# Queries and keys of an attention stage formed by seven half-block products instead of eight full ones, with the work around them reordered

## The chip, the core and the metric

The kernel runs as one program on one core of a Trainium2 chip. The metric is the device time in microseconds; three runs of the kernel before gave 2507.08, 2508.03 and 2508.86 us, median 2508.03. All data is float32. The engines are called as the profile calls them: PE (TensorE: the matrix products, with PEld for its weight loads), DVE (VectorE), ACT (ScalarE), POOL (GpSimd) and SP (the engine that issues most transfers).

## The reference

Four layers act on `x` of 128 x 64 x 256 (batch, node, feature) with one adjacency matrix of 64 x 64. Each adds its result to `x`; each starts with a layer norm and a relu. The first is a graph convolution followed by small LSTMs, the second is attention, the third a graph layer with two batch norms, the fourth three graph convolutions. Only the attention matters here:

```python
qkv = h @ W                                   # h: relu(layernorm(x)), W: 256 x 768
q, k, v = ...                                 # four heads of 64
mask = jnp.where(adj == 0, -jnp.inf, 0.0)
scores = einsum('bhid,bhjd->bhij', q, k) / np.sqrt(64) + mask
attn = jax.nn.softmax(scores, axis=-1)
x = x + einsum('bhij,bhjd->bhid', attn, v)
```

## The kernel before, in words

The 8192 tokens (128 batches of 64 nodes) are cut into 16 groups (`NG`) of 512 tokens (`GN`). The program is written engine by engine through a tile layer: within an engine the instructions run in the order in which the layer issues them, engines wait for each other by semaphores, and `tc.issue_after(...)` says that what follows may not be issued ahead of a named instruction. All products go through eight PSUM banks from one pool (`psp`, `bank()`).

**The attention loop** (L843 to L892) takes one group for each turn `g`, with pieces of neighbouring groups between:

- `to_residual(g + 3)` (L236, transposes at L246, additions at L250) brings the first layer's result of a later group into `xs`, by way of a copy `hc` made half by ACT and half by POOL (L239).
- `queries_keys(hT)` (L735) multiplies the transposed features `hT` (256 features on 2 x 128 partitions, 512 tokens) by the 256 x 512 weights `wqk`: four output tiles of 128 x 512, two products each, eight products 512 columns wide (L744), and ACT copies each result into `q` or `k` (L748).
- `values(hT, v, (0,))` and later `(1,)` (L760, copy L766) make the values, 16 narrow products for each half.
- `turn(e)` (L808, copies L811) transposes the exponentials of the group before.
- `features(transposed(h))` (transposes L124, copies by DVE at L258) makes the `hT` of the next group.
- `attend` (L821) makes the outputs of the group before, and `softmax` (L768) the scores of this group (L779), mask and scale (L786), maximum (L793), subtraction (L794), the exponential on ACT (L795), and their sums and reciprocals on DVE (L798, L799).
- `add_output(g - 1)` (L833 on DVE, L836 on POOL) divides by the sums and adds to `xs`; `normalized(g + 2)` (bn_stats L90, L92, L93, the power on POOL at L94, L96, the four activations L109 on ACT) prepares a later group's `h`.

After group 15 the loop's last turn runs into the third layer: `mixed` (L141) and `hidden` (L716), whose weights `w1` come by a transfer (L863) into the place of `wqk`.

**The seven-product form** exists already in the kernel: the LSTM gates and the fourth layer use it. A product of two matrices, each cut into 2 x 2 blocks, is formed from seven block products instead of eight; `sums` and `differences` form the combined blocks, four tensor operations each, and `seven` (L159) issues the products in the order 1, 5, 6, 7 into four banks. ACT copies products 1 and 5 to `p1`, `p5` (L169, L170), DVE adds products 6 and 7 to these (L172, L173), and then `finish` adds p1 and p5 on POOL for one output block (L176) and issues products 2, 3 and 4 on top of banks whose first contents have been read. One block is then read out by ACT (L210), two by DVE (L181, L185).

**Before the attention** come the LSTM steps. In the last of them `w_att` is loaded with the attention's weights (L668), and group 0's `hT` is made between LSTM products (L683). The last LSTM output `h` is written at L538, after a tanh at L530.

Of the kernel before, what the change touches and what calls it, by code (L numbers as in the profile page):

```python
# [14 lines left out]
P = 128  # L15
D = 256
# [22 lines left out]
def adj_preln_kernel(ctx: ExitStack, tc: tile.TileContext, x_in, adj, vec, bg0, bg1,  # L39
# [9 lines left out]
    def bank(shape=(P, 512)):  # L49
        return psp.tile(list(shape), F32, tag="ps", name="ps")  # L50
# [68 lines left out]
    def transposed(src):  # L119

        pss = [bank() for _ in range(2)]
        for c in range(2):
            for t in range(GT):
                nc.tensor.transpose(  # L124
                    pss[c][:, t * P : (t + 1) * P], src[:, t, c * P : (c + 1) * P], ident
                )
        return pss
# [32 lines left out]
    def seven(products, banks, p1, p5, out, end, parts=lambda b: [b]):  # L160

        ps = banks
        for i, p in zip((1, 5, 6, 7), ps):
            products[i](p, True)
        nc.scalar.copy(p1, ps[0])  # L169
        nc.scalar.copy(p5, ps[1])  # L170

        nc.vector.tensor_tensor(p1, p1, ps[2], ALU.add)  # L172
        nc.vector.tensor_tensor(p5, p5, ps[3], ALU.add)  # L173

        def finish():
            nc.gpsimd.tensor_tensor(out=out[1][1], in0=p1, in1=p5, op=ALU.add)  # L176
            end(1, 1, None)
            products[2](ps[0], False)
            end(0, 0, ps[0])
            products[3](ps[1], False)  # L180
            nc.vector.tensor_tensor(out[0][1], p1, ps[1], ALU.add)  # L181
            end(0, 1, None)
            products[4](ps[3], False)
            for to, p, q in zip(*(parts(b) for b in (out[1][0], p1, ps[3]))):
                nc.vector.tensor_tensor(to, p, q, ALU.add)  # L185
                end(1, 0, None, to)

        return finish

    def differences(eng, b11, b12, b21, b22, t1, t2, t3, t4, negate=False):  # L190
# [61 lines left out]

    keep = ctx.enter_context(tc.tile_pool(name="keep", bufs=1))

    def features(pss, k):

        for c in range(2):
            nc.vector.tensor_copy(hTs[:, k, c, :], pss[c])  # L258
        return hTs[:, k]

    with tc.tile_pool(name="lw", bufs=5) as lw:

# [201 lines left out]
        with tc.tile_pool(name="back", bufs=1, reuse_waits="tile") as back_pool, \  # L464
# [183 lines left out]
            for p, nk in ((1, 8), (2, 8), (3, 7), (4, 8)):  # L648
                n = nk * HB
                wi, wh = w_next  # L650
                if p < 4:
                    w_next = (load_w(wih, p), load_w(whh, p))
                starts = range(0, NODES // p // nk * nk, nk)
                units = [(tiles, k0) for tiles in ((0, 1), (2, 3)) for k0 in starts]

                for j in range(0, len(units), 2):
                    two = [unit(p, *u, nk) for u in units[j : j + 2]]
                    first_steps(p, n, two, units[j : j + 2], w0)
                    if p > 1:
                        flush()  # L660
                        if j == 0:
                            ws = blocks_of(p, wi, wh)
                    if j + 2 == len(units):
                        if p < 4:
                            w0 = first_blocks(w_next[0], weight_tile())
                        else:
                            w_att = weight_tile()
                            nc.sync.dma_start(  # L668
                                out=w_att[:, :, 0:768], in_=wqkv.rearrange("(c p) f -> p c f", p=P)
                            )  # L670
                            wqk, wv = w_att[:, :, 0:512], w_att[:, :, 512:768]
                    for t in range(1, p):
                        for i, u in enumerate(two):
                            next_step(t, p, n, u, ws)

                            if p == 4 and j == 2 and 2 * t + i - 2 < NK:
                                to_residual(2 * t + i - 2, xs[2 * t + i - 2], back_pool, 1)
                            if p == 4 and j == 2 and t == p - 1 and i == 0:

                                h = back_pool.tile([P, GT, D], F32, tag="hc", name="h")  # L680
                                ln_relu(xs[0], h)
                                hTs = keep.tile([P, 2, 2, GN], F32, tag="arena", name="hT")
                                hT = features(transposed(h), 0)  # L683

    xpool_b = ctx.enter_context(tc.tile_pool(name="xres_b", bufs=1, reuse_waits="tile"))
    for g in range(NK, NG):
# [42 lines left out]
    with tc.tile_pool(name="att", bufs=2, reuse_waits="tile") as ap_:  # L729
# [2 lines left out]
            ln_relu(xs[g], h)  # L732
            return h

        def queries_keys(hT):  # L735

            qk = []
            for s, tag in enumerate(("q", "k")):
                dst = ap_.tile([P, 2, GN], F32, tag=tag, name=tag)
                for m in range(2):  # L740
                    ps = bank()
                    col = s * D + m * P
                    for c in range(2):
                        nc.tensor.matmul(  # L744
                            ps, lhsT=wqk[:, c, col : col + P], rhs=hT[:, c, :],
                            start=(c == 0), stop=(c == 1),
                        )
                    nc.scalar.copy(dst[:, m, :], ps)  # L748
                qk.append(dst)
            return qk  # L750

        def values(hT, v, ks):

# [14 lines left out]
        def softmax(qT, kT):  # L768


            e = ap_.tile([P, 2 * GT, 2, NODES], F32, tag="e", name="e")
            pss = [bank((P, 2 * GT, NODES)) for _ in range(2)]
            for t in range(GT):
                for m in range(2):
                    for b in range(2):
                        tok = t * P + b * NODES
                        for par in range(2):
                            rows = slice(par * 64, par * 64 + 64)
                            nc.tensor.matmul(  # L779
                                pss[par][b * 64 : b * 64 + 64, 2 * t + m, :],  # L780
                                lhsT=qT[rows, m, tok : tok + NODES],
                                rhs=kT[rows, m, tok : tok + NODES],
                                start=True, stop=True,
                            )
            for par in range(2):
                nc.vector.scalar_tensor_tensor(  # L786
                    e[:, :, par, :], pss[par], 0.125,
                    mask.unsqueeze(1).to_broadcast([P, 2 * GT, NODES]), ALU.mult, ALU.add,
                )
            ef = e.rearrange("p a q j -> p (a q) j")  # L790
            NH = 4 * GT
            mx = ap_.tile([P, NH, 1], F32, tag="mx", name="mx")
            nc.vector.tensor_reduce(mx[:, :, 0], ef, AX.X, ALU.max)  # L793
            sub = nc.vector.tensor_tensor(ef, ef, mx.to_broadcast([P, NH, NODES]), ALU.subtract)  # L794
            nc.scalar.activation(ef, ef, AF.Exp)  # L795
            ri = ap_.tile([P, 2 * GT, 2, 1], F32, tag="ri", name="ri")
            rif = ri.rearrange("p a q o -> p (a q o)")
            nc.vector.tensor_reduce(rif, ef, AX.X, ALU.add)  # L798
            nc.vector.reciprocal(rif, rif)  # L799
            return e, ri, sub.ins  # L800

        def turn(e):

# [34 lines left out]

        h = normalized(1)
        last = None
        for g in range(NG + 1):  # L843
            if 0 < g <= NG - NK:
                to_residual(g + NK - 1, xs[g + NK - 1], ap_, 1)
            if g == NG - NK + 1:
                hres_pool.__exit__(None, None, None)
                with tc.using_default_side("right"):
# [6 lines left out]
                    mixed(i, (on_scalar, on_scalar))  # L855
                hidden(0, w1, range(2))
            if g < NG:
                q, k = queries_keys(hT)
                if g == NG - 1:

                    w1 = w_att[:, :, 0:512]
                    w2 = w_att[:, :, 512:1024].rearrange("p a (b f) -> a p b f", f=D)
                    nc.sync.dma_start(out=w1, in_=w1t.rearrange("(c p) f -> p c f", p=P))  # L863
                v = ap_.tile([P, 2 * GT, P], F32, tag="v", name="v")
                values(hT, v, (0,))
            if last is not None:
                e, ri, v_last = last
                eT, turned = turn(e)
# [1 line left out]
                with tc.issue_after(sub), tc.issue_after(turned):  # L870
                    activated(ar_right, 1)
            if g < NG:
                values(hT, v, (1,))
            else:
                counted = hidden(0, w1, range(2, 4))
            if g + 1 < NG:
                hT = features(transposed(h), (g + 1) % 2)
            if last is not None:
                pss = attend(eT, v_last)
            if g < NG:  # L880
                e, ri_next, sub = softmax(q, k)
                last = (e, ri_next, v)
                with tc.issue_after(sub):
                    if g > 0:
                        add_output(g - 1, pss, ri)
                    if g + 2 < NG:
                        h = normalized(g + 2)
                    elif g + 2 == NG:
                        activated(ar_right, 0)
            else:  # L890
                add_output(g - 1, pss, ri)
                after_attention = sub  # L892
# [376 lines left out]
```

## Time and profile before

| What | Value |
|---|---|
| median of three runs | 2508.03 us |
| the profiled execution: time, span | 2508.48 us, 2506.70 us |
| PE busy | 2473.8 us, 99% of the span |
| DVE, ACT, POOL busy | 1458.3, 1137.7, 419.1 us |
| attention stage, L744 first to last start | 1219.5 to 1459.2 us |
| L744: 256 PE records, 128 x 512 | 112.8 us busy, 593 ns each |
| L258: hT copies of DVE in 1215 to 1475 us | x30, 19.3 us, 686 ns each |
| L748: q and k copies of ACT | x64, 37.1 us, 584 ns each |
| mean granted clock of TensorE | 0.996 |

The busy time of PE counts records that overlap, so the distance from the start of one group of products to the start of the next tells what they cost. A float32 product shows as two records in the trace: eight products of L744 for each group, 256 records in 16 groups. "Idle before" in a row is the time for which the engine stood still just before these instructions, and the releaser is what ended it.

### The profile page before, as it was taken

What the parts mean: (1) busy time and instruction counts of PE and PEld (TensorE: products, weight loads), DVE (VectorE), ACT (ScalarE), POOL (GpSimd) and SP (SyncE); (2) the same over time, 40 slices, a digit from 0 to 9 for tenths busy, and PEclk for the clock granted to TensorE, in tenths of its full rate; (3) what the DMA queues carried; (4) which work ended last, traced back from release to release, by engine and by line L of the source; (5) the groups of instructions that cost most, each with busy time, mean ns of one, the idle gap of its engine ahead of it and who ended that gap; (6) DMA issues with size and microseconds to landing.
All of it is one profiled execution on the core that took longest, in us unless ns stands there. A gap on an engine that the chain in (4) does not pass through costs nothing.

```text
span 2506.7 us, 46889 instructions
## 1 busy us (share of the span) xinstructions
PE 2473.8 (99%) x20190; PEld 2044.8 (82%) x20190; DVE 1458.3 (58%) x2616; ACT 1137.7 (45%) x2011; POOL 419.1 (17%) x352
## 2 busy tenths in 40 slices
PE   8999999999999999999999999998999999999999
PEld 6668888889999998888766654445898888888888
DVE  6658876666566575565566676425555454554544
ACT  4547754444444343444555466653333333333332
POOL 4422211111111111111133221003111101111110
PEclk9999999999999999999999999998999999999999
DMA  3200000000000000000300000010000000000000
GB/s 115 102 2 1 1 18 1 1 1 34 1 1 1 1 1 1 1 13 1 102 2 2 2 19 1 1 59 1 10 10 10 18 10 10 18 10 10 18 10 18
DMA packets 30095, 39.64 MB, mean 16 GB/s; under 512 B 1600, under 2 KB 26304, under 8 KB 29888
## 3 DMA queue, kind: packets, MB, share of 16 engines
q1 hardware_dynamic: 29184, 36.09, 4.3%
q8 instruction: 158, 2.59, 0.4%
q10 hardware_dynamic: 704, 0.56, 0.1%
q14 instruction: 49, 0.40, 0.1%
HBM read 28.26 MB, written 8.39 MB: 15 GB/s over the span
## 4 chain that ended last, share of the span: by engine, by line
PE 93%; DVE 3%; ACT 1%; POOL 1%; issue 1%; DMA 0%; DVEq 0%; ACTq 0%; POOLq 0%
PE ps L497 40%; PE ps L1083 15%; PE ps L1128 8%; PE ps L744 4%; PE ps L975 4%; PE ps L716 4%; PE ps L141 4%; PE ps L1047 3%; PE ps L419 2%; PE ps L760 2%; PE ps L443 2%; PE ps L821 1%; PE ps L124 1%; ACT arena L213 1%; PE ps L246 1%
## 5 line engine op out<-in xcount | busy, mean ns | idle before, releaser
L497 PE MATMUL ps<-diff,s 128*128 128x256 f32 (+1 forms) x1824 | 393.5, 371 | 0.9 <-DVE diff L613 0.9
L1083 PE MATMUL ps<-arena 128*128 128x256 f32 x1792 | 392.7, 381 | 1.2 <-DVE arena L194 1.2
L1083 PEld LDWEIGHTS ps<-arena 128*128 128x128 f32 x1792 | 337.9, 190 | 55.4 <-issue 10.9
L497 PEld LDWEIGHTS ps<-diff,s 128*128 128x128 f32 x1824 | 345.9, 190 | 33.8 <-issue 1.6
L511 ACT ACTIVATE gates<-gates,lbias 128x512 f32<-128x512 f32 (+5 forms) x426 | 244.2, 621 | 203.4 <-DVE gates L181 146.3
L176 POOL TENSOR_TENSOR gates<-p 128x512 f32<-128x512 f32 (+1 forms) x115 | 148.6, 1292 | 883.1 <-DVE p L173 832.0
L497 PE MATMUL ps<-h,w 128*128 128x256 f32 (+1 forms) x1028 | 241.3, 371 | 1.6 <-ACT p L169 1.6
L497 PE MATMUL ps<-diff,w 128*128 128x256 f32 (+1 forms) x1040 | 238.7, 370 | 0.0
L497 PEld LDWEIGHTS ps<-diff,w 128*128 128x128 f32 x1040 | 197.4, 190 | 18.2
L497 PEld LDWEIGHTS ps<-h,w 128*128 128x128 f32 x1028 | 194.7, 190 | 20.9 <-ACT p L169 2.0
L511 ACT ACTIVATE gates<-ps,lbias 128x256 f32<-128x256 f32 (+3 forms) x213 | 91.6, 476 | 247.4 <-PE ps L497 247.3
L213 ACT ACTIVATE arena<-arena 128x512 f32<-128x512 f32 (+1 forms) x160 | 88.6, 582 | 192.4 <-POOL arena L176 103.6
L176 POOL TENSOR_TENSOR arena<-arena 128x512 f32<-128x512 f32 x64 | 73.3, 1145 | 535.5 <-DVE arena L173 535.5
L1128 PE MATMUL ps<-arena 128*128 128x128 f32 x1280 | 149.9, 276 | 0.0
L1128 PEld LDWEIGHTS ps<-arena 128*128 128x128 f32 x1280 | 145.6, 192 | 1.3 <-issue 0.2
L181 DVE TENSOR_TENSOR gates<-p,ps 128x512 f32<-128x512 f32 (+1 forms) x115 | 76.5, 665 | 119.7 <-PE ps L497 119.7
L181 DVE TENSOR_TENSOR arena<-arena,ps 128x512 f32<-128x512 f32 x64 | 39.7, 622 | 149.1 <-PE ps L1083 84.4
L94 POOL TENSOR_TENSOR rstd<-rstd,mhalf 128x4 f32<-128x4 f32 (+1 forms) x66 | 66.4, 1006 | 306.5 <-DVE rstd L93 306.4
L497 PE MATMUL ps<-state,w 128*128 128x256 f32 (+1 forms) x512 | 116.1, 370 | 0.9 <-ACT p L169 0.8
L497 PE MATMUL ps<-state,s 128*128 128x256 f32 (+1 forms) x512 | 115.8, 369 | 0.0
L185 DVE TENSOR_TENSOR gates<-p,ps 128x512 f32<-128x512 f32 (+1 forms) x115 | 76.8, 668 | 64.6 <-PE ps L497 63.9
L716 PE MATMUL ps<-arena,w 128*128 128x512 f32 x256 | 114.0, 598 | 0.0
(189 smaller groups left out, 3923.5 us busy)
## 6 DMA issues: line engine op xcount, KB each, us to landing
x<-in_x SPq DMA_DIRECT2D x27, 512.0 KB, 6.9
out<-x SPq DMA_DIRECT2D x15, 512.0 KB, 2.9
w<-in_wih SPq DMA_DIRECT2D x4, 1024.0 KB, 7.3
w<-in_whh SPq DMA_DIRECT2D x3, 1024.0 KB, 6.2
arena<-in_l3w SPq DMA_DIRECT2D x3, 1024.0 KB, 5.3
w<-in_wqkv SPq DMA_DIRECT2D x1, 768.0 KB, 4.3
x<-in_x SPq DMA_DIRECT2D x2, 256.0 KB, 3.1
wg<-in_wg ACTq DMA_DIRECT2D x2, 256.0 KB, 6.3
```

The costliest lines, as they stand in the source:

```text
L141: nc.tensor.matmul(pss[b][half * 64 : half * 64 + 64, c, t, :], lhsT=src[rows, t, col : col + 64], rhs=a2[rows, :], start=True, stop=True,)
L176: nc.gpsimd.tensor_tensor(out=out[1][1], in0=p1, in1=p5, op=ALU.add)
L181: nc.vector.tensor_tensor(out[0][1], p1, ps[1], ALU.add)
L185: nc.vector.tensor_tensor(to, p, q, ALU.add)
L213: nc.scalar.activation(o, o, func)
L497: nc.tensor.matmul(ps[:, r], lhsT=wc[:, j, :], rhs=bc, start=first and r == 0 and c == 0, stop=True, skip_group_check=True,)
L511: nc.scalar.activation(o, ps, func, bias=lbias[:, col : col + 1])
L716: nc.tensor.matmul(ps, lhsT=w1[:, c, m * P : (m + 1) * P], rhs=a[:, 2 + c, :], start=(c == 0), stop=(c == 1),)
L744: nc.tensor.matmul(ps, lhsT=wqk[:, c, col : col + P], rhs=hT[:, c, :], start=(c == 0), stop=(c == 1),)
L975: nc.tensor.matmul(pss[m], lhsT=w2[c // 2][:, c % 2, m * P : (m + 1) * P], rhs=a[:, c, :], start=(c == 0), stop=(c == 3),)
L1083: nc.tensor.matmul(ps[:, r, :], lhsT=w[:, c, col : col + P], rhs=b[:, c, :], start=first and r == 0 and c == 0, stop=c == 1, skip_group_ch ...
L1128: nc.tensor.matmul(ps[:, t, :], lhsT=w[:, c, t * P : (t + 1) * P], rhs=b[:, c, :], start=first and t == 0 and c == 0, stop=c == 3, skip_gr ...
```

## The change

In `queries_keys` the weights are cut into four blocks of 128 x 256 (features by outputs) and the features into four of 128 x 256 (features by tokens). Seven block products, each made of two products 256 columns wide, take the place of eight products 512 columns wide. Their combined weights are formed once: two of the four in the LSTM phase, into the unused last quarter of `w_att`, and two (`wsum`) just ahead of the attention loop. The combined features are formed for each group: `features` now copies by ACT and then issues four DVE operations 128 x 256. The buffers `q`, `k` have one copy instead of two.

In the loop the first half of the values now stands ahead of the products of queries and keys, `turn` stands between products 7 and 2, and `to_residual` stands after the second half of the values. `add_output` of a group and the sums of its exponentials are issued one turn later, behind the second of the additions in `seven` (`finish.behind`). The load of `w1` in the last group follows `finish`.

```diff
-        nc.vector.tensor_tensor(p5, p5, ps[3], ALU.add)
+        added = nc.vector.tensor_tensor(p5, p5, ps[3], ALU.add)
...
+        finish.behind = added.ins
         return finish
...
-    def features(pss, k):
+    def features(pss):
+        hT, t = hTs[:, 0], hTs[:, 1].rearrange("p a (b n) -> p (a b) n", n=HN)
         for c in range(2):
-            nc.vector.tensor_copy(hTs[:, k, c, :], pss[c])
-        return hTs[:, k]
+            nc.scalar.copy(hT[:, c, :], pss[c])
+        blocks = [[hT[:, c, n * HN : (n + 1) * HN] for n in range(2)] for c in range(2)]
+        ts = [t[:, i] for i in range(4)]
+        differences(nc.vector, *blocks[0], *blocks[1], *ts, negate=True)
+        return hT, (*blocks, ts)
...
+                            ss = [w_att[:, c, 768:1024] for c in range(2)]
+                            nc.vector.tensor_tensor(ss[0], wqk[1][0], wqk[1][1], ALU.add)
+                            nc.vector.tensor_tensor(ss[1], ss[0], wqk[0][0], ALU.subtract)
...
-        def queries_keys(hT):
-            qk = []
-            for s, tag in enumerate(("q", "k")):
-                dst = ap_.tile([P, 2, GN], F32, tag=tag, name=tag)
-                for m in range(2):
-                    ps = bank()
-                    col = s * D + m * P
-                    for c in range(2):
+        def queries_keys(b):
+            q, k = qk = [ap_.tile([P, 2, GN], F32, tag=t, name=t, bufs=1) for t in ("q", "k")]
+            p15 = ap_.tile([P, 2, 2, HN], F32, tag="p15", name="p15", bufs=1)
+            def product(w, x):
+                def issue(ps, first):
+                    for r in range(2):
                         nc.tensor.matmul(
-                            ps, lhsT=wqk[:, c, col : col + P], rhs=hT[:, c, :],
-                            start=(c == 0), stop=(c == 1),
+                            ps[:, r, :], lhsT=w[:, r * P : (r + 1) * P], rhs=x,
+                            start=first and r == 0, stop=True, skip_group_check=True,
                         )
-                    nc.scalar.copy(dst[:, m, :], ps)
-                qk.append(dst)
-            return qk
+                return issue
+            out = [[d[:, :, n * HN : (n + 1) * HN] for n in range(2)] for d in qk]
+            finish = seven(
+                sevens(wqk_blocks, b, product), [bank((P, 2, HN)) for _ in range(4)],
+                p15[:, 0], p15[:, 1], out, ends_in(out, AF.Copy),
+            )
+            return q, k, finish
...
-            nc.vector.tensor_reduce(rif, ef, AX.X, ALU.add)
-            nc.vector.reciprocal(rif, rif)
-            return e, ri, sub.ins
+            def sums_of():
+                nc.vector.tensor_reduce(rif, ef, AX.X, ALU.add)
+                nc.vector.reciprocal(rif, rif)
+            return e, ri, sub.ins, sums_of
...
+        wsum = ap_.tile([P, 2, D], F32, tag="wsum", name="wsum", bufs=1)
+        nc.vector.tensor_tensor(wsum[:, 0], wqk[0][0], wqk[1][0], ALU.subtract)
+        nc.vector.tensor_tensor(wsum[:, 1], wqk[0][1], ss[1], ALU.subtract)
+        wqk_blocks = (*wqk, ss + [wsum[:, 0], wsum[:, 1]])
...
         for g in range(NG + 1):
-            if 0 < g <= NG - NK:
-                to_residual(g + NK - 1, xs[g + NK - 1], ap_, 1)
...
             if g < NG:
-                q, k = queries_keys(hT)
-                if g == NG - 1:
-                    w1 = w_att[:, :, 0:512]
...
-                    nc.sync.dma_start(out=w1, in_=w1t.rearrange("(c p) f -> p c f", p=P))
+                hT_all, blocks = hT
                 v = ap_.tile([P, 2 * GT, P], F32, tag="v", name="v")
-                values(hT, v, (0,))
+                values(hT_all, v, (0,))
+                q, k, finish = queries_keys(blocks)
+            if last is not None:
+                with tc.issue_after(finish.behind):
+                    if g > 1:
+                        add_output(g - 2, pss, ri)
+                    sums_of()
...
             if g < NG:
-                values(hT, v, (1,))
+                finish()
+                if g == NG - 1:
+                    w1 = w_att[:, :, 0:512]
...
+                    nc.sync.dma_start(out=w1, in_=w1t.rearrange("(c p) f -> p c f", p=P))
+                values(hT_all, v, (1,))
...
+            if 0 < g <= NG - NK:
+                to_residual(g + NK - 1, xs[g + NK - 1], ap_, 1)
             if g + 1 < NG:
-                hT = features(transposed(h), (g + 1) % 2)
+                hT = features(transposed(h))
...
                 with tc.issue_after(sub):
-                    if g > 0:
-                        add_output(g - 1, pss, ri)
```

More of the change, by code (lines that the diff above doesn't have):

```diff
@@ L670, in adj_preln_kernel @@
                             )
-                            wqk, wv = w_att[:, :, 0:512], w_att[:, :, 512:768]
+                            wqk = [[w_att[:, c, m * D : (m + 1) * D] for c in range(2)] for m in range(2)]
+                            wv = w_att[:, :, 512:768]
+                            ss = [w_att[:, c, 768:1024] for c in range(2)]
+                            nc.vector.tensor_tensor(ss[0], wqk[1][0], wqk[1][1], ALU.add)
+                            nc.vector.tensor_tensor(ss[1], ss[0], wqk[0][0], ALU.subtract)
                     for t in range(1, p):
@@ L682, in adj_preln_kernel @@
                                 hTs = keep.tile([P, 2, 2, GN], F32, tag="arena", name="hT")
-                                hT = features(transposed(h), 0)
+                                hT = features(transposed(h))
     xpool_b = ctx.enter_context(tc.tile_pool(name="xres_b", bufs=1, reuse_waits="tile"))
@@ L857, in adj_preln_kernel @@
             if g < NG:
-                q, k = queries_keys(hT)
-                if g == NG - 1:
-                    w1 = w_att[:, :, 0:512]
-                    w2 = w_att[:, :, 512:1024].rearrange("p a (b f) -> a p b f", f=D)
-                    nc.sync.dma_start(out=w1, in_=w1t.rearrange("(c p) f -> p c f", p=P))
-                v = ap_.tile([P, 2 * GT, P], F32, tag="v", name="v")
-                values(hT, v, (0,))
+                hT_all, blocks = hT
+                v = ap_.tile([P, 2 * GT, P], F32, tag="v", name="v")
+                values(hT_all, v, (0,))
[5 more added lines that the diff above has]
+                    sums_of()
             if last is not None:
@@ L872, in adj_preln_kernel @@
             if g < NG:
-                values(hT, v, (1,))
+                finish()
+                if g == NG - 1:
+                    w1 = w_att[:, :, 0:512]
+                    w2 = w_att[:, :, 512:1024].rearrange("p a (b f) -> a p b f", f=D)
+                    nc.sync.dma_start(out=w1, in_=w1t.rearrange("(c p) f -> p c f", p=P))
+                values(hT_all, v, (1,))
             else:
                 counted = hidden(0, w1, range(2, 4))
+            if 0 < g <= NG - NK:
+                to_residual(g + NK - 1, xs[g + NK - 1], ap_, 1)
             if g + 1 < NG:
-                hT = features(transposed(h), (g + 1) % 2)
+                hT = features(transposed(h))
             if last is not None:
@@ L880, in adj_preln_kernel @@
             if g < NG:
-                e, ri_next, sub = softmax(q, k)
+                e, ri_next, sub, sums_of = softmax(q, k)
                 last = (e, ri_next, v)
                 with tc.issue_after(sub):
-                    if g > 0:
-                        add_output(g - 1, pss, ri)
                     if g + 2 < NG:
```

## The prediction

> **What bounds the kernel now.** I read the page's busy shares first, then the stretches of the attention stage, then PE's order of time in one group.
>
> ```profile
> PE 2473.8 (99%) x20190; PEld 2044.8 (82%) x20190; DVE 1458.3 (58%) x2616; ACT 1137.7 (45%) x2011; POOL 419.1 (17%) x352
> ```
>
> ```profile
> core 0: us, PE busy (x) PEld busy (x) DVE busy (x) ACT busy (x) POOL busy (x), PEclk, DMA share, GB/s
> 1268.00:1284.00 16.00, 16.00 (x234) 11.15 (x233) 10.62 (x23) 8.47 (x14) 4.70 (x4) 1.00 0.01 1
> 1710.00:1720.00 10.00, 5.40 (x16) 2.63 (x14) 6.97 (x23) 2.35 (x4) 1.55 (x3) 0.82 0.00 1
> 1720.00:1730.00 10.00, 7.15 (x75) 5.65 (x76) 5.64 (x18) 4.40 (x7) 0.97 (x2) 0.50 0.01 2
> ```
>
> In a 16 us stretch of attention PE is never idle, DVE works 10.62 us, ACT 8.47, POOL 4.70. A group costs what PE's products cost, and time is won only there. (The last two rows, from another stage, are used below.) One group on PE:
>
> ```profile
> 1303.64 2.02 PE L760 MATMUL ps<-w,hT 128*64 128x128 f32 x32
> 1305.59 1.09 PE L808 MATMUL ps<-ident,e 128*128 128x128 f32 x8
> 1306.61 2.02 PE L760 MATMUL ps<-w,hT 128*64 128x128 f32 x32
> 1308.56 1.09 PE L124 MATMUL ps<-ident,h 128*128 128x128 f32 x8
> 1309.59 1.16 PE L821 MATMUL ps<-v,eT 64*64 64x64 f32 x64
> 1310.57 1.11 PE L779 MATMUL ps<-k,q 64*64 64x64 f32 x64
> 1311.61 1.09 PE L246 MATMUL ps<-ident,hc 128*128 128x128 f32 x8
> 1312.54 7.03 PE L744 MATMUL ps<-hT,w 128*128 128x512 f32 x16
> 1319.50 0.76 PE L760 MATMUL ps<-w,hT 128*64 128x128 f32 x9
> ```
>
> Start to start: each half of the values 1.95 us, turn 1.02, next features 1.03, attend 0.98, scores 1.04, residual 0.93, queries and keys 6.96. Sum 15.86 us a group.
>
> **What the Trainium skill says.** "TensorE: Matmul & The Clock Gate", What's actually happening: PE's clock falls to half after an idle window of about 3.4 us, and windows run free of the kernel. The trace agrees: PE worked 5.40 of 10 us and the clock then stood at 0.50. "GPSIMD Engine Reference", Specifications: POOL shares its SBUF interfaces with VectorE, and contends with DVE instructions that have two SBUF inputs. It agrees too: beside a POOL addition at 1078.16 us (1.56 us, others 1.27) a DVE subtraction of this kind took 1.76 us instead of 0.69. "ScalarE: Activation LUTs", What ACT_TABLE_LOAD costs: activations back to back overlap by about 93 ns. Here copies of 0.58 us follow at 0.48.
>
> **The change part by part.**
>
> Products. Removed for each group: eight products, 6.96 us. Added: 14 of 256 columns. The LSTM's L497 has this shape: eight records, four products, go from 1217.81 to 1219.54 us, so 0.432 us each; 14 take 6.05. PE also changes once more between kinds of products: +0.05, an estimate from the 0.07 by which 6.96 exceeds 16 records of 0.4306. Gain 0.86 a group, **13.8 us** for 16.
>
> DVE, each group: minus two copies (0.6 each of its time), plus four subtractions of 128x256 (0.42, the rate of L185 in that size), plus two additions and two read-outs of 128x512 (L833's 0.684, 0.6 in sequence). About 13.5 us of 15. ACT loses four copies, gains two of features and three from `seven`: 9.0 us. POOL gains one L176, 1.3: 6.0 us. All three stay below PE, so order decides. I walk one group through the built order of each queue, with 0 at the end of its scores on PE.
>
> - PE up to the turn: values 1.95, products 1, 5, 6, 7 at 0.865: it wants the exponentials at 5.41.
> - ACT before 0: residual transposes end at -3.05. Its `hc` copy (1.20) starts 0.2 later and stands ahead of both hT copies, which end at -1.17 and -0.69.
> - DVE: four subtractions from -1.13; DVE is free at 0.46. Mask and scale twice to 1.75, maximum (1.22) to 2.99, subtraction to 4.24.
> - ACT: copy of product 5 starts 0.2 after it ends, 3.88; the exponential (1.06) follows at 4.36, ends 5.42. PE waits about **0.1**.
> - DVE goes on: bn_stats and their rest to 5.7, the two additions to 7.1, POOL's power waited for to 7.6, outputs twice to 8.9, sums to 10.0, read-outs to 11.5, residual additions, behind PE, to 12.9.
> - PE: turn to 6.5, products 2, 3 to 8.25, product 4 (needs the second addition, 7.1), values to 11.05, residual, features, attend, scores at 14.0 (needs the last read-out, 11.5). POOL's L176 (7.1 to 8.4), then outputs of 1.27 each end by 11.5, ahead of its `hc` copy at 12.2.
>
> So outputs and sums, moved past the additions, stand ahead of both read-outs, and still leave 2.5 us. They cost nothing, covered by PE's values, residual, features and attend. Group period 15.06 against 15.86. In 13 groups of this kind 1.3 us is lost to the exponential. Bounds 0 and 0.5 a group.
>
> The start. In group 0 product 7 needs `wsum`, and both operations for it stand on DVE behind the last LSTM outputs:
>
> ```profile
> 1224.94 1.29 DVE L538 TENSOR_TENSOR h<-gates 128x512 f32<-128x512 f32 x2 [1.18 <-ACT gates L530]
> 1219.54 7.03 PE L744 MATMUL ps<-hT,w 128*128 128x512 f32 x16
> ```
>
> PE starts attention at 1219.54: values to 1221.49, products 1, 5, 6 to 1224.08. `wsum` can only begin at about 1226.2 and takes 0.42: 1226.65. Before, PE had products of 7 us here that needed none of this. **PE stands 2.6 us**, and half the values, products 2 to 4 are queued behind. Above: 3.7, if POOL's copy of the LSTM result (L239, 1226.39 before, 1.08 us) delays the DVE operation. Below: 2.2, if DVE starts `wsum` as soon as L538's second half issues.
>
> Elsewhere. The two weight sums in the LSTM phase: the transfer, issued at 1069.45, lands 4.3 us later, and DVE reaches them at about 1074.8, after L586: no wait, 0.84 us in a phase where PE is full and DVE has gaps. ACT's copies for group 0 likewise. SP: the same transfers; only `w1` of the last group moves, behind product 4; it lands 3.7 us after about 9 us of a turn whose end first reads it at 17. Last group: two layer norms stand ahead of the read-outs on DVE, attend waits about 2 us where it waited 1.03; 0.96 that PE then idled is covered. Net 0, bounds -1 and +1.
>
> Sum: -13.8 + 1.3 + 2.6 = **-9.9 us** on 2508.48 of the profiled execution (span 2506.70, 1.78 around it): 2498.6. The median of the runs is 0.45 lower: 2498.1.
>
> **The rivals.** The measurement can tell about 0.2%, 5.0 us, from no change.
>
> 1. As above: 2498.1, own range 2494 to 2502. Chance 0.55.
> 2. *The clock falls.* The halt of 2.6 us falls into one free-running window or two. In the trace the window of 3.41 us before the fall had PE 20% busy; one of 56% at 170 us brought none. The halt leaves between 24 and 62%. The one fall seen lasted from 1716.4 to 1730.0, 13.65 us; at half rate that costs 6.8 us: 2504.9; two windows, 3.4: 2501.5. For it: nothing else here idles PE as long in attention. Against: most positions leave more than 20%. Chance 0.22.
> 3. *DVE and ACT hold PE a little in each group.* DVE goes from 10.6 to 13.5 of 15 us and 0.1 us of slack lies on the exponential. With 0.5 us a group, 2503. Chance 0.14.
> 4. *Slower: POOL's copy holds the subtractions.* If `hc` on POOL (1.20) runs when DVE wants its four subtractions with two SBUF inputs, as beside L613, then mask, exponential and turn come 1.2 us later for 12 groups, and hT's subtractions are next late: 14.4 us more, 2512.5. It decides from 0.85 us a group (9.9 plus 1.3, over 13). Against: POOL's copy ends about -1.6, DVE starts at -1.13. Chance 0.09, with other waits of that size.
>
> That the products are not fewer is excluded by the built order: 14 of 128x256 for eight of 128x512.
>
> **The numbers.** Predicted: 2498.1. Range 2493.5 to 2507: all of 1 and 2, most of 3; what lies outside is 4. Faster by over 5.0 us is below 2503.0: nearly all of 1, a third of 2, half of 3: 0.68. Within: 0.23. Slower: 0.09.
>
> **What would show it.** Right: products 128x256 at 0.216 us a record; a period near 15.1 us; one halt of PE near 1224 to 1226.7, released by DVE's `wsum`; waits of the turn on L810's exponential of about 0.1; DVE near 13.5 in 15 us. Wrong: PE waiting on DVE's L193 to L197 or on ACT's features in each group; DVE without gaps; a PEclk of 0.5 near 1230; PE idle at product 4 or scores.

## The result, and the profile after

The changed kernel takes **2499.54 us** (median of 7 runs, 2498.49 to 2501.57) against 2508.43 (7 runs) of the kernel before: a ratio of 0.9967, 95% interval 0.9955 to 0.9979. Run again beside the experiments it took 2501.12 (6 runs) against 2508.30, ratio 0.9970 (0.9958 to 0.9982). The forecast was 2498.1. The profiled execution took 2501.02 us, with a span of 2498.9.

The page's busy shares, and then the stretches (columns: the stretch and its length, busy time of PE, PEld, DVE, ACT and POOL, granted clock, DMA share, GB/s). The first stretch is one group long, the other two are the start of attention:

```profile
PE 2461.4 (98%) x20382; PEld 2078.8 (83%) x20382; DVE 1518.5 (61%) x2716; ACT 1148.1 (46%) x2027; POOL 440.1 (18%) x368
```

```profile
1267.10:1282.20 15.10, 15.10 (x246) 13.26 (x248) 14.17 (x29) 9.04 (x15) 6.03 (x5) 1.00 0.01 2
...
1225.00:1230.00 5.00, 3.47 (x23) 2.80 (x25) 3.90 (x6) 4.13 (x8) 2.07 (x2) 0.71 1.07 353
1230.00:1235.00 5.00, 5.00 (x34) 4.07 (x31) 1.38 (x2) 1.04 (x2) 0.30 (x1) 0.95 1.09 348
```

PE is still never idle within a group, but DVE went from 10.62 of 16 us to 14.17 of 15.10, not to the 13.5 that was forecast. PE's order of time in one group:

```profile
1311.16 1.11 PE L794 MATMUL ps<-k,q 64*64 64x64 f32 x64
1312.20 2.02 PE L775 MATMUL ps<-w,hT 128*64 128x128 f32 x32
1314.15 2.86 PE L753 MATMUL ps<-hT,w 128*128 128x256 f32 x12
1316.85 1.03 PE L753 MATMUL ps<-hT,wsum 128*128 128x256 f32 x4
1317.79 1.09 PE L826 MATMUL ps<-ident,e 128*128 128x128 f32 x8
1318.72 1.03 PE L753 MATMUL ps<-hT,w 128*128 128x256 f32 x4
...
1326.23 1.11 PE L794 MATMUL ps<-k,q 64*64 64x64 f32 x64
```

Scores to scores it is 15.07 us (1311.16 to 1326.23), where it was 15.86. Start to start, 12 records of products 1, 5 and 6 take 2.70 us, 0.225 each with the change between kinds, and the four records of product 2, like those of product 3, 0.86 to 0.87, 0.216 each: a record costs what the LSTM's row had said.

The waits of PE in attention (engine, operand and line; what it waited for; us in total, times, longest) and the start on PE:

```profile
PE ps L753 <- DVE wsum L862: 2.3, 1, 2.3
PE ps L794 <- DVE k L185: 1.7, 1, 1.7
PE ps L725 <- ACT arena L153: 0.5, 1, 0.5
PE ps L826 <- ACT e L810: 0.2, 1, 0.2
```

```profile
1221.40 2.86 PE L753 MATMUL ps<-hT,w 128*128 128x256 f32 x12
1226.53 1.53 PE L753 MATMUL ps<-hT,wsum 128*128 128x256 f32 x4 [2.28 <-DVE wsum L862]
1228.00 3.15 PE L775 MATMUL ps<-w,hT 128*64 128x128 f32 x28
```

The halt for `wsum` is there, 2.28 us. Behind it product 7 takes 1.47 us, start to start, instead of 0.87, and the values are slow as well: the clock fell. From the two stretches above, (0.29 + 0.05) x 5 us of clock are missing, so it stood at half for 3.4 us and 1.7 us were lost.

Where the 7.8 us between the spans lie, by starts on PE:

| Stretch | before | after | difference | forecast |
|---|---|---|---|---|
| start of attention to its first scores | 11.67 | 16.02 | +4.35 | +1.74 (-0.86 + 2.6) |
| 14 periods, scores to scores | 220.44 | 210.24 | -10.20 | -10.7 (14 x -0.86 + 1.3) |
| last group, scores to first `hidden` | 19.42 | 18.78 | -0.64 | -0.86, bounds of 1 |
| all else | | | -1.3 | 0 |

Of the last row 0.66 us lie in the next 10 us after that, where a wait of 0.60 us of the kernel before for ACT's L109 is gone; the other 0.6 is spread and unexplained.

### The profile page after: what moved, and what is told of

Its sections match the earlier page's. It is cut to its first block, busy times and chain, and to the rows that moved or that the text cites. A ratio compares the mean times of both kernels' runs of the same rounds, so it can differ in the third digit from the quotient of the medians.

```text
span 2498.9 us, 47547 instructions
## 1 busy us (share of the span) xinstructions
PE 2461.4 (98%) x20382; PEld 2078.8 (83%) x20382; DVE 1518.5 (61%) x2716; ACT 1148.1 (46%) x2027; POOL 440.1 (18%) x368
## 4 chain that ended last, share of the span: by engine, by line
PE 91%; DVE 4%; ACT 2%; POOL 1%; issue 1%; DMA 0%; DVEq 0%; SPq 0%; POOLq 0%; ACTq 0%
PE ps L502 40%; PE ps L1112 16%; PE ps L1157 8%; PE ps L725 4%; PE ps L1004 4%; PE ps L141 4%; PE ps L753 3%; PE ps L1076 3%; PE ps L424 2%; PE ps L775 2%; PE ps L448 2%; ACT arena L214 1%; PE ps L247 1%; PE ps L839 1%; PE ps L826 1%
## 5 line engine op out<-in xcount | busy, mean ns | idle before, releaser
L176 POOL TENSOR_TENSOR gates<-p 128x512 f32<-128x512 f32 (+1 forms) x115 | 149.3, 1298 | 882.1 <-DVE p L173 831.0
L176 POOL TENSOR_TENSOR arena<-arena 128x512 f32<-128x512 f32 x64 | 72.9, 1138 | 535.5 <-DVE arena L173 535.5
L172 DVE TENSOR_TENSOR p<-p,ps 128x512 f32<-128x512 f32 (+1 forms) x131 | 86.9, 663 | 50.9 <-PE ps L502 50.3
L185 DVE TENSOR_TENSOR gates<-p,ps 128x512 f32<-128x512 f32 (+1 forms) x115 | 76.8, 668 | 64.2 <-PE ps L502 63.5
```

## Experiments

The theory from the trace: PE bounds each group, the gain is PE's, and the start gives part of it back. Its rival: DVE is by now a second bound, and the places of copies, outputs and sums decide whether PE's saving shows at all.

**The changed kernel again.**

> The changed kernel once more, unaltered. In its first profile PE halted 2.3 us for wsum at 1224 us and the clock then stood at half for one window of 3.4 us (about 1.7 us lost); its seven times lay in two groups, near 2499.1 and near 2501.3 us. Theory 1: the fall of the clock is drawn anew in each execution (where the halt lies against the free-running windows), and that makes the two groups: median 2499 to 2501, and a new profile shows the halt of 2.3 us again, with or without a PEclk below 1 behind it. Theory 2: the fall is in every execution; then the profile shows it again and the groups come from elsewhere.

Measured: 2501.12 us (2499.47 to 2502.30). The halt is again 2.28 us and the clock fell behind it again:

```profile
1225.00:1230.00 5.00, 3.85 (x32) 3.50 (x32) 3.50 (x6) 3.73 (x7) 2.38 (x2) 0.77 1.08 360
1230.00:1235.00 5.00, 5.00 (x26) 3.77 (x24) 1.37 (x2) 1.43 (x3) 0.00 (x0) 0.89 1.09 347
```

That is (0.23 + 0.11) x 5 / 0.5 = 3.4 us at half once more. But in the profile of `e8_last_group`, described below, the same halt of 2.28 us, with the same products ahead of it, brought no fall; the same two stretches of it:

```profile
1225.00:1230.00 5.00, 3.47 (x35) 2.89 (x36) 3.88 (x6) 4.14 (x8) 2.07 (x2) 1.00 1.07 354
1230.00:1235.00 5.00, 5.00 (x89) 4.06 (x88) 2.18 (x5) 2.26 (x4) 0.30 (x1) 1.00 1.09 348
```

So the fall comes in some executions and not in others, as theory 1 said: of the eight profiles here that have this halt, five show the fall, 3.4 us of half clock each time, and three do not. `e8_last_group` also prices it: from the first product to the first scores the same instructions take 12.46 us there and 14.07 in the first profile, 1.6 us more.

What differs is where the halt lies on a grid of 3.41 us. Falls begin and end on this grid: in the first profile the one above begins at 1227.06 us and ends at 1230.47, and a later one begins at 1708.34, which is 141 such steps after the first. In the window of the grid that holds most of the halt, PE's records fill 33, 45, 33, 33 and 39% in the five profiles with the fall (the changed kernel, `e0_after_again`, `e2_old_place`, `e11_nmr_pool_features_dve`, `e13_two_fewer_nmr_pool`) and 47, 52 and 59% in the three without (`e8_last_group`, `e3_features_dve`, `e5_two_fewer`). This orders windows around the same work and is no threshold for other work: in the kernel before a fall at 19.94 us follows a window that PE's records fill to 72%.

That the fall makes the two groups of times (2499.3 and 2501.5 on average over 13 runs, 2.2 apart) fits the three profiles named so far, which lie in the upper, upper and lower group of their kernels. It is not shown. In a later stage, near 1710 us, the clock falls in all three as well, for 13.65 us in the first two and for 10.24 in `e8_last_group`, so this difference fits the groups just as well. In `e11_nmr_pool_features_dve` the clock fell behind the halt too, and its profiled time of 2499.98 lies in the lower part of its runs. And 25 runs of the kernel before, which has no such halt, spread over 3.0 us (2507.32 to 2510.29).

**No halt at the start.**

```diff
+    s3 = wqk[1][0]                       # in the LSTM phase
+    nc.vector.tensor_tensor(s3, wqk[0][0], s3, ALU.subtract)
...
+    if g == 0:
+        values(hT_all, v, (1,))
     finish()
```

> The first of the two operations that make wsum is done in the LSTM phase (over the weight block that only the sums still read), and in group 0 alone the second half of the values goes ahead of products 2 to 4. Nothing is left out. Theory 1 (PE bounds, the halt is a pure loss): no wait of PE at product 7, PEclk 1.00 there, so 2.3 us less in every execution and 1.7 us more in those in which the clock fell: 2495.5 to 2497, and one group of times. Theory 2 (the halt is covered, or comes back at product 2, at product 4 or at the first scores, since DVE is as late as before with everything behind it): within 0.7 us of the changed kernel, 2499 to 2501.

Measured: 2497.99 us (2496.80 to 2498.32), 3.1 less than the changed kernel in the same comparison; ratio to before 0.9958 (0.9946 to 0.9971). On PE:

```profile
1221.38 3.72 PE L755 MATMUL ps<-hT,w 128*128 128x256 f32 x16
1225.03 2.02 PE L777 MATMUL ps<-w,hT 128*64 128x128 f32 x32
...
1231.92 1.16 PE L796 MATMUL ps<-k,q 64*64 64x64 f32 x64 [1.26 <-DVE k L185]
```

No halt at product 7 and no fall of the clock, but 1.26 us come back at the first scores: the values that stood between product 4 and the scores, and hid the read-outs, have been used up earlier. POOL has a part in it: L193, the first subtraction of the next features, stands ahead of the read-outs on DVE and took 1.47 us instead of 0.42 beside POOL's L176. Both theories hold a part. 2.28 - 1.26 of waiting and the clock's 1.7 make 2.7; the first scores start 3.2 us earlier than in the repeated run (1231.92 against 1235.08).

**Read-outs ahead of a layer norm in the last group**, alone and with the edit above.

```diff
-    with tc.issue_after(sub), tc.issue_after(turned):
-        activated(ar_right, 1)           # ahead of finish()
+    with tc.issue_after(finish.read):    # the last read-out on DVE
+        activated(ar_right, 1)           # after finish()
```

> Only the order on DVE in the last group changes: the layer norm of group 1 after attention is queued behind the last read-out, not ahead of it. The wait of 1.70 us of the last scores on DVE's read-out should fall to under 0.5 us. Theory 1 (the last group's wait is a loss of its own): 1.2 us less, 2498.3 if the changed kernel runs at 2499.5. Theory 2 (the prediction's: net nothing, another wait is next late): the products of the mixed features of group 1 wait for the layer norm that now stands later, or for ScalarE's copies as they did by 0.49 us; within 0.5 us of the changed kernel.

> Both edits: no halt in group 0 and the last group's read-outs ahead of the layer norm. Theory 1: the gains add, 2494.3 to 2496. Theory 2: the gain of the first edit alone, 2495.5 to 2497. If neither wait was on the path: 2499 to 2501.

Measured: 2500.66 us (2500.35 to 2502.09) beside 2501.12 for the changed kernel, and 2498.31 (2497.43 to 2499.68) for both edits beside 2497.99 for the first alone. Nothing gained. In the waits of `e8_last_group` the 1.7 us on L185 are gone, and others stand in their place:

```profile
PE ps L141 <- issue: 0.9, 1, 0.9
...
PE ps L141 <- ACT arena L109: 0.4, 1, 0.4
```

The time moved from one wait to others: from the last but one scores to the first `hidden` it is 19.52 us, not less than the 18.78 of the changed kernel. Theory 2 holds, as the prediction had it. In the profile of `e9_both` the clock fell for one window at 1459.69 us, among these waits; what that took from a gain is not shown.

**Outputs and sums in their old place**, the rest of the change kept.

```diff
-    with tc.issue_after(finish.behind):  # next turn, behind the additions
-        if g > 1:
-            add_output(g - 2, pss, ri)
-        sums_of()
...
     e, ri_next, sub, sums_of = softmax(q, k)
+    sums_of()
...
+        if g > 0:
+            add_output(g - 1, pss, ri)   # behind sub, ahead of normalized(g + 2)
```

> Seven products kept, features by ScalarE kept, but outputs and sums of a group stand on DVE where they stood before the change: ahead of the two additions. Theory 1 (the prediction's walk: the additions would end at about 9.6 us after the scores, and product 4 is wanted at 8.25): PE waits about 1.3 us at product 4 in each of 14 groups, +18 us, about 2517; the change without the move would have been slower than before. Theory 2 (DVE's slack takes it, the move is worth nothing): 2499 to 2501.

Measured: 2520.84 us (2520.40 to 2521.81), ratio to before 1.0049 (1.0035 to 1.0062), nearer to theory 1, and above it. The move is worth about 20 us; without it the change would have made the kernel slower. The period is 16.54 us. In the order of DVE the second addition ends at 1327.35, and PE's product 4 starts at 1327.46, right behind it:

```profile
1322.01 1.28 DVE L851 TENSOR_TENSOR o<-ps,ri 128x512 f32<-128x512 f32 x2
1323.21 0.41 DVE L90 BATCH_NORM_STATS2 st<-x 128x6 f32<-128x256 f32 x1
1323.54 1.20 DVE L815 TENSOR_REDUCE ri<-e 128x16 f32<-128x1024 f32 x1
...
1326.67 0.68 DVE L173 TENSOR_TENSOR p<-p,ps 128x512 f32<-128x512 f32 x1
```

The built order gave PE 20 records of values to do before product 4, so a wait is recorded there only once (0.2 us), but the values, now split around product 4, take 2.48 us, start to start, instead of 1.95. The layer norm's `h`, late behind the same operations, holds the next features (L124 took 1.53 us, start to start, for 0.97).

**Feature copies back on DVE**, and with them one operation moved to POOL. In the changed kernel's DVE one row stands out:

```profile
1318.79 0.68 DVE L173 TENSOR_TENSOR p<-p,ps 128x512 f32<-128x512 f32 x1
1320.02 1.22 DVE L96 SCALAR_TENSOR_TENSOR nmr<-mv,rstd 128x4 f32<-128x4 f32 x1 [0.55 <-POOL rstd L94]
```

```profile
1318.97 1.02 POOL L94 TENSOR_TENSOR rstd<-rstd,mhalf 128x4 f32<-128x4 f32 x1 [8.19 <-DVE rstd L93]
1319.96 1.27 POOL L176 TENSOR_TENSOR k<-p 128x512 f32<-128x512 f32 x1
```

L96 works on 128 x 4 numbers and takes 1.22 us; in the kernel before its median was 0.163. It runs for as long as POOL's new addition L176, which starts with it. The first line below is of the kernel before. The second is of the changed kernel's last group, where POOL's next operation starts only 0.88 us after the power:

```profile
1306.14 0.16 DVE L96 SCALAR_TENSOR_TENSOR nmr<-mv,rstd 128x4 f32<-128x4 f32 x1 [1.13 <-POOL rstd L94]
```

```profile
1461.21 0.17 DVE L96 SCALAR_TENSOR_TENSOR nmr<-mv,rstd 128x4 f32<-128x4 f32 x1 [0.61 <-POOL rstd L94]
```

There L96 has waited 0.61 us for the power and still takes 0.17. So the wait does not lengthen it; what is new beside the long rows is the addition.

```diff
-    nc.scalar.copy(hT[:, c, :], pss[c])
+    nc.vector.tensor_copy(hT[:, c, :], pss[c])
```

> Only the two feature copies of each group go back from ScalarE to VectorE. Theory 1 (DVE has no room left: 14.17 of 15.10 us in the changed kernel's stretch, about 1.05 of it a wait for POOL, and two copies of 0.6 us more): DVE needs about 15.3 us a group, PE waits for the exponentials or the scores 0.2 to 0.4 us a group, +3 to +6 us, 2503 to 2506. Theory 2 (the copies are covered, or the wait for ScalarE's copies goes as well): within 1 us of the changed kernel, about 2499.5.

Measured: 2508.99 us (2508.14 to 2510.73), no faster than the kernel before (ratio 1.0002, 0.9994 to 1.0011). The loss is larger than theory 1's, its mechanism the same: DVE has no gap left but the one before L96, its cycle is 15.79 us, and PE waits in each group:

```profile
PE ps L826 <- ACT e L810: 7.7, 13, 0.6
```

Then the same with the mean times rstd formed by POOL, between its power and L176:

```diff
+    nc.vector.tensor_scalar(nmr, mv[:, :, 0], -1.0, None, ALU.mult)
     ...                                  # variance on DVE, power on POOL, as before
-    nc.vector.scalar_tensor_tensor(nmr, mv[:, :, 0], -1.0, rstd, ALU.mult, ALU.mult)
+    nc.gpsimd.tensor_tensor(out=nmr, in0=nmr, in1=rstd, op=ALU.mult)
```

> The feature copies on VectorE, as in e3_features_dve, and in attention's layer norm the mean times rstd is formed on POOL, right behind its power, ahead of L176 (VectorE only negates the mean, 128x4). In the changed kernel this operation (L96, 128x4) took 1.22 us on VectorE in each group, 0.16 in the kernel before, beside POOL's L176, after 0.55 us of waiting for POOL. Theory 1 (POOL's L176 holds L96 by the shared SBUF port, and this hold is what makes VectorE a second bound): VectorE's cycle falls from the 15.79 us of e3_features_dve by about 1.6 us to 14.2, under PE's 15.07; the waits of the turn on the exponentials (7.7 us in 13) go; 2499 to 2502, although the copies are on VectorE. Theory 2 (the 1.22 us is not POOL's doing, or the chain of the exponentials is late for the copies themselves): 2507 to 2510 as in e3_features_dve.

Measured: 2500.18 us (2499.49 to 2502.49), with a period of 15.06 us and no wait for the exponentials. On POOL the operation costs 0.20 us:

```profile
1318.60 1.02 POOL L96 TENSOR_TENSOR rstd<-rstd,mhalf 128x4 f32<-128x4 f32 x1 [8.28 <-DVE rstd L95]
1319.69 0.20 POOL L98 TENSOR_TENSOR nmr<-nmr,rstd 128x4 f32<-128x4 f32 x1
1319.84 1.27 POOL L181 TENSOR_TENSOR k<-p 128x512 f32<-128x512 f32 x1
```

It gives back all that the copies had cost, so the hold and the wait before it were what made DVE a second bound. This edit takes both away together; it does not say how much each was worth alone.

**Two products left out**, without and with that edit.

```diff
+    products[2] = products[3] = lambda ps, first: None
```

> Products 2 and 3 of the seven are left out, so queries and keys are wrong by these terms; every addition, read-out and copy stays. Four records of 256 columns less in each group, 0.86 us. Theory 1 (PE bounds and DVE has about 1 us of room, as predicted with 13.5 of 15): 13.8 us less, 2485.7, with a period of 14.2 us. Theory 2 (DVE's 14.17 of 15.10 us is a bound just below PE): the period stops near 14.6 to 15 us, 2 to 8 us less, 2492 to 2498, and PE waits on DVE.

> Products 2 and 3 left out as in e5_two_fewer (queries and keys lack these terms), and the mean times rstd on POOL. Without the second edit the period stopped at 14.60 us and PE waited 0.57 us a group for the exponentials. Theory 1 (VectorE's own cycle of 14.6 us was the bound there, 1.6 of it the wait for POOL and the held L96): PE bounds again with a period of 14.2 us, 2486 to 2488. Theory 2 (something else sets 14.6 us): 2492 to 2494 as in e5_two_fewer.

Measured: 2493.04 us (2491.78 to 2494.34) and 2485.46 (2484.98 to 2485.92). The expectation for the first counts four records for what is left out. That is wrong: products 2 and 3 have four records each, so eight go, 1.73 us of PE's work in each group and 27.7 us in all (PE has 20254 records instead of 20382, 128 fewer in 16 groups). With PE as the only bound the period would be 15.07 - 1.73 = 13.34 us.

The first saves only 6.5 to 8 us against the two medians of the changed kernel, with a period of 14.60 us, and PE waits for the exponentials:

```profile
1290.40 1.11 PE L796 MATMUL ps<-k,q 64*64 64x64 f32 x64
...
1305.00 1.11 PE L796 MATMUL ps<-k,q 64*64 64x64 f32 x64
```

```profile
PE ps L828 <- ACT e L812: 6.3, 10, 1.5
```

In such a period DVE has no gap but the 0.55 us before L96. So DVE's own cycle was 14.60 us, 0.47 below PE's 15.07. Theory 2 held. Once DVE is relieved, 14 to 16 us are saved, and the period is 13.99 us:

```profile
1291.46 1.11 PE L802 MATMUL ps<-k,q 64*64 64x64 f32 x64
...
1305.45 1.11 PE L802 MATMUL ps<-k,q 64*64 64x64 f32 x64
```

This confirms that L96 and the wait before it had set the 14.60 us. But it is not theory 1's case, whose 14.2 us come from the wrong count: 13.99 is 0.65 above 13.34, though DVE now has a gap of 0.8 to 0.9 us in each period. PE's rows show no wait in it but are longer, start to start, than in the changed kernel: product 7 takes 1.09 us (0.94), the turn 1.02 (0.93), the values, split around product 4, 2.26 (1.95), and product 4 1.06 (0.95). What makes them longer stays open.

**All of the change but the products**, and so without the combined features and weights.

```diff
     # ScalarE copies features, outputs and sums a turn later, residual after the products;
-    q, k, finish = queries_keys(blocks)
+    q, k = queries_keys(hT)              # eight products of 512 columns
```

> All of the change but the products: features copied by ScalarE, outputs and sums one iteration later, residual after the products, but queries and keys by the eight products of 512 columns as before. Theory 1 (PE alone bounds; the order is worth nothing by itself): within 1.5 us of the kernel before, 2507 to 2510, with groups of 15.86 us. Theory 2 (part of the gain is the order's): 2500 to 2505.

Measured: 2511.08 us (2509.17 to 2512.74), ratio to before 1.0010 (1.0002 to 1.0018): just outside theory 1's range, on the slow side. The order by itself wins nothing. Its periods mostly alternate between 15.8 and 16.15 us; the waits that the trace lists for PE (0.8 us there) do not account for it, and this stays open. Against this kernel the seven products are worth 10 to 11.5 us.

**The best version**: no halt, and POOL's operation.

> e1_no_halt (first half of wsum in the LSTM phase, values of group 0 ahead of products 2 to 4) and the mean times rstd on POOL; feature copies on ScalarE. Theory 1 (PE alone bounds the groups in the middle, so 1.6 us less on VectorE in each group is worth nothing there; only waits on VectorE at the two ends shorten, 1.26 us at the first scores and 1.70 at the last): 0 to 1.5 us less than e1_no_halt's 2497.99. Theory 2 (VectorE still costs a little in each group): 3 us less or more, below 2495.

Measured: 2496.32 us (2495.79 to 2497.50), ratio to before 0.9953 (0.9941 to 0.9966): faster than the kernel before by 12 us, and every run of it below every run of the changed kernel. Its median lies 1.7 us below that of the first edit alone (the runs of the two overlap: 2495.79 to 2497.50 and 2496.80 to 2498.32), a little more than theory 1 allowed, and not where theory 1 put it: the waits at the two ends are as long as they were.

```profile
PE ps L802 <- DVE k L190: 3.0, 2, 1.7
```

Apart from the first period, the changed kernel has three of 15.24, 15.49 and 15.35 us instead of 15.07, 0.9 us more in all, and the first edit alone three of 15.28, 15.41 and 15.31; here only one is left (15.24), and in `e11_nmr_pool_features_dve` none. That is 0.6 of the 1.7 us; the rest is not located. The longer periods went with DVE's load, though PE's rows show no wait in them, only slower values (32 records in 2.38 us instead of 1.95, start to start). How DVE's load would slow them is not shown.

## Why the prediction was right, and where it was not

The time was right (-8.9 us between the medians against -9.9), and most of the terms:

- **Products, -0.86 us a group.** Right: 0.216 us a record, period 15.07 against the walk's 15.06. Luck made the sum so exact. From the first to the end of the last, start to start, the seven products take 6.32 us; the forecast was 6.10, and the exponential's share below makes it 6.17. The turn (0.93 instead of 1.02) and the next features (0.97 instead of 1.03) give the 0.15 back, which nothing forecast. The 14 periods gained 10.2 us of the 10.7 forecast.
- **Exponential, 0.1 us a group.** Right in kind: one wait of 0.2 us was recorded, and in the group shown the exponential ends at 1317.74, just ahead of the turn at 1317.79, which starts 0.94 us after product 7 where four records take 0.87. Some 0.9 us were lost in three longer periods instead.
- **Outputs and sums cost nothing where they stand now.** Right, and `e2_old_place` shows the reason: the old place costs 20 us.
- **The halt for `wsum`, 2.6 us.** Right. The trace calls 2.28 us idle, counting from the modelled end of product 6; by the rate of the records it is 1226.53 - 1223.99 = 2.54. The upper bound by POOL's copy was not reached: it held only the second of the two operations (1.31 us for 0.42), which product 7 does not need.
- **The clock (rival 2).** Given 0.22, it happened in both profiles of the changed kernel, for one window: 1.7 us in each profiled execution. Where it happens it would more than account for the 1.0 us by which the gain falls short of the forecast. Of the 2.6 us by which the start exceeds its forecast it is 1.6: without a fall, in `e8_last_group`, the start took 14.41 us. The other 1.0 lies in slower rows; the values of the second half, split into 28 and 4 records, take 2.47 us there instead of 1.95. The prediction's "one fall seen" overlooks the one at 19.94 us in the same trace, which lasted 6.83 us.
- **Last group, net 0.** Right within its bounds (-0.64 for -0.86), by another road: the wait stood at the scores (1.70 us), not at attend.
- **DVE, "about 13.5 of 15".** This step failed, while ACT (9.04 us) and POOL (6.03) came as forecast. The trace shows 14.17, and `e5_two_fewer` a cycle of 14.60. The missing term is L96: priced at 0.16 us as it stood in the kernel before, it takes 1.22 beside POOL's L176, which the change puts right behind the power that L96 waits for. The walk could have shown it, but gave POOL two things at once: the power up to 7.6 and L176 from 7.1 to 8.4. One behind the other, L176 starts just when L96 does. Rival 4 had the right mechanism, POOL holding a DVE operation with two inputs in SBUF, and looked for it at the `hc` copy; "GPSIMD Engine Reference" of the Trainium skill (Specifications) states this sharing, and here it costs 1.06 us a group. It cost little only because 0.47 us of room was left. The prediction reached the right sum with a margin on DVE three times too wide (1.5 us of 15), and that was luck: with the feature copies still on DVE, +1.2 us, the same sum stays below PE's and would have called the change a gain of 10 us where `e3_features_dve` shows none.
- **Elsewhere, 0.** Measured -1.3, of which 0.66 is a wait of the kernel before that is gone.

## What to carry to other kernels

When work is taken off the engine that bounds a loop, sum the next engine's cycle with its waits and holds, not only its operations: here PE's saving was 0.8 us a group, and DVE's cycle ended 0.47 us below what was left. An operation's price belongs to its neighbours in time; when the change puts a POOL operation beside it, take the price of a held row and not that of the row before. One-off work at the entry of a pipelined stage belongs in the stage before, and what then waits next should be looked up before counting the whole halt as won.

## What was not expected of the hardware

- A DVE operation on 128 x 4 numbers took 1.22 us instead of 0.163 beside a POOL addition of two SBUF inputs (128 x 512, 1.27 us): it ended with POOL's operation. Two subtractions of 128 x 256, usually 0.42 us, show the same: 1.31 us beside a POOL copy of 1.11 us (L863, at the start) and 1.47 beside the addition (L193, in `e1_no_halt`). Each ended within 0.3 us of POOL's operation, so in these rows the hold goes by POOL's length and not by DVE's size.
- A single halt of PE of 2.28 us was enough for one window of 3.4 us at half clock in some executions and brought none in others, with the same instructions around it. "TensorE: Matmul & The Clock Gate" of the Trainium skill (What's actually happening) speaks of an idle window; here the window before the fall held work as well, since the halt is shorter than it: PE's records filled 33 to 45% of it where the clock fell and 47 to 59% where it did not.
- Falls of the clock near 20 us come and go between executions. In the one pair compared they cost nothing up to attention: with one, the repeated run reached its first products of queries and keys no later (1221.01 us) than the profile without one (1221.40).
